# The last batch's attention in two passes of queries, with three quarters of its expert routing beside the second pass

## The chip, the cores and the metric

The kernel runs on one core of one Trainium2 chip. All arithmetic is in 32-bit floats. The metric is the device time of the whole kernel in microseconds (us): the median of the runs shown is 2341.13 us (three runs, 2332.34 to 2346.16).

## What is computed

Four batches of 2048 tokens, 256 features, go through an attention layer and a layer of experts, each between two layer norms, with a residual. Cut to what matters:

```python
# attention, per batch and head (16 heads of 16): z are 1-number projections of keys and queries
out_i = sum_j max(0, 1 - |z_i - z_j| / b_h) * v_j          # then / T
x = x + layernorm(out)
# experts: 8192 tokens h = layernorm(x), 64 experts, top 8, capacity 128 per expert in token order
shared = (silu(h @ Wg) * (h @ Wu)) @ Wd * sigmoid(h @ w_gate)   # width 512
probs = softmax(h @ gate_w); w, idx = top_k(probs, 8); w = w / sum(w)
y = sum over the 8 of  w * expert_e(h)      # only where the token is among the first 128 of expert e
x = x + layernorm(y + shared)
```

The capacity is handed out in token order over all batches, so an expert's list is only known when every token ahead has been routed.

## The kernel before, in words

**Foreground: attention.** A unit `t` of the loop at the end of `sandwich_kernel` is one head `h` and one tile `s` of 128 keys against all 2048 queries of a batch; there are `NU` = 256 units a batch, 1024 in all, and 64 units (4 heads, 16 key tiles) make a phase. For a unit, `score` writes `hat` = |q + k| over 128 keys x 2048 queries on ScalarE (L1558), or with two VectorE instructions (L1553, L1555) when VectorE's account `spare` is in credit; then VectorE makes min(hat, 1) - 1 (L1562). `product` multiplies `hat` by the head's values on TensorE (L1588): four matmuls a unit, each 128 keys x 32 value columns x 512 queries, one per block `c` of 512 queries. A matmul uses only 32 of the array's 128 columns, those of quarter `j`, the unit's head within its phase; block `c` is issued `c` units late, so that the four matmuls of one turn of the loop (units t, t-1, t-2, t-3) lie in four different quarters:

```python
def product(t):
    for c in range(4):
        tt = t - c
        ...
        nc.tensor.matmul(pa[k, c][32 * j:32 * j + 32, :], lhsT=vt[b, s]..., rhs=hat[tt][0][:, c * BK:(c + 1) * BK], ...)
```

After 128 units (8 heads) `evict` moves the four accumulators from PSUM to a tile `ct`, which goes to DRAM (`cx_d`) in batches 0 to 2 and stays in SBUF in batch 3. Queries are loaded broadcast to all partitions by `load_q` (L1539, 512 KB each), from 13 buffers called "big" that the hats share.

**Background: a planner.** Everything else is queued as small tasks in the class `Background`, in one list whose order is the priority. `bg.step()` is called once a unit. It goes through the list and emits each task whose predecessors are some steps old (`LAG`), whose buffers are free ("slot", "bank", "half"), and whose engine has budget left. Budgets are in us of the planner's own costs per step: `CAP` is 0.88 for TensorE, 0.75 for VectorE and 0.4 for ScalarE from batch 2 on. Each engine runs what it is given in the order given. `bg.flush(tasks)` emits the named tasks, and all that they depend on, at once and without regard to age. `bg.drain()` runs the planner alone after the attention, with a budget of 1.0.

**What is queued, and when.** `finish(b)` is queued 8 units into batch b + 1, for b = 0 to 2. It has the parts `front(c)` for four chunks of 512 tokens (load, transposes, layer norms, gate logits), `tail()` (softmax, top 8 and the codes of the tokens, 128 x 64 each, transposed into `scT`), `keep` (L706), `first` (L713 and L715: rounds of MAX8 and MATCH_REPLACE8 over `scT` that pick the earliest tokens) and `shared(c)`, the shared expert of a chunk: 16 matmuls of 512 columns (L573), Silu (L587), products (L589), 16 matmuls of 256 columns (L602), and a store of the result to `y_d` (L619). A matmul in 32-bit floats is two records in the trace, so a chunk of the shared expert is 32 records of each kind. `early` queues the 64 experts of the first half of the tokens (L1041 gather, L1047 to L1064, L1066 scatter with addition), ahead of `finish(2)` in the list. The "slot" buffers are ten; four of them go to the experts and are not handed back.

**After the attention.** Batch 3's own `finish` is written by hand: `front_last` (L721 to L891) for its four chunks, then `keep`, `first` over 1088 columns, `merge` (L963, L965), `ranking` (L1096 to L1186), and 15 items of experts for the second half (`item`: gather L1217, matmuls L1223 to L1240, 28 scatters L1258). All of these scatters add into `y_d` on top of the shared expert of batch 2, so they wait for its stores:

```python
rest, bg.q = bg.q, []          # what the attention left over
...
bg.q = mine + rest             # mine: front_last, keep, first, merge, ranking
ys = stored[2]
... item(env, i, late + [i_] + ..., ks, ys, wl[i])
outs = shared_last(env, exps, gates, xts)      # shared expert of batch 3 (L911 to L938)
```

Last come the `final` tasks of 16 chunks (L1281 load of `y_d`, L1288 to L1307 layer norm, L1321 addition to the output): eight need only the first half's experts, eight wait for the last item's scatter.

Of the kernel before, what the change touches and what calls it, by code (L numbers as in the profile page):

```python
# [25 lines left out]
class Background:  # L26
# [8 lines left out]
    def __init__(self, make):  # L35
        self.make = make
        self.free = {}
        self.q = []
        self.t = 0
        self.debt = dict.fromkeys(self.CAP, 0.0)  # L40
        self.spent = dict.fromkeys(self.CAP, 0.0)
        self.alone = False
# [27 lines left out]
    def emit(self, k):  # L70
        for key, r in k.get.items():
            tag, _ = self.free[r].pop(0)
            k.env[key] = self.make(tag)
            k.env["tag", key] = (r, tag)
# [66 lines left out]
def sandwich_kernel(ctx: ExitStack, tc: tile.TileContext, x_in, wqT, bq, wkT, bk, wvT, bv, wprojT, log_bw,  # L141
# [38 lines left out]
    cx_d = [dram.tile([NG, P, T], F32, name=f"cx_d{b}") for b in range(B - 1)]  # L180
# [5 lines left out]
    ysh_d = dram.tile([T, F], F32, name="ysh_d")  # L186
# [28 lines left out]
    NS = NT // 2 * P  # L215
    scT = const.tile([P, NS + CAP], F32, name="scT")
# [9 lines left out]
    with ExitStack() as ph:  # L226
# [31 lines left out]
        bg = Background(make)  # L258
        bg.free["slot"] = [(f"s{i}", 0) for i in range(NSLOT)]
# [196 lines left out]
        def finish(b, after=()):  # L456
# [5 lines left out]
            xfree = []  # L462
            def front(c):
# [93 lines left out]
                a = bg.add("act", 0.25, gate, [a])  # L557
                gts = bg.add("dve", 0.1, lambda gt=gt: nc.vector.tensor_scalar(gt, gt, 0.5, 0.5, ALU.mult, ALU.add), [a])
                ready[c] = (done, gt, gts)

            def shared(c):
# [32 lines left out]
                for i2 in range(2):  # L594
# [15 lines left out]
                    if i2 == 0:  # L610
# [10 lines left out]
                                 yy, put=[] if b == NE else [ys], env=env)  # L621
                stored[b].append(free_ys)
                if b == NE:
                    bg.add("sp", 1.0, lambda ys=ys, c=c: nc.sync.dma_start(rows(ysh_d, c * CT, CH), chunkview(env[ys])),
                           [free_ys], put=[ys], env=env)

            def tail():


                lgv = lambda: env["lg"].rearrange("p (n e) -> p n e", e=E + 1)[:, :, :E]  # L630
                mkv = lambda: env["lg"][:, :NT * E].rearrange("p (n e) -> p n e", e=E)
                prv = lambda: env["pr"][:, :NT * E].rearrange("p (n e) -> p n e", e=E)
                mx = t8 = ts_ = None
                t0 = b * NT
                wide = lambda a: a.unsqueeze(2).to_broadcast([P, NT, E])

                def most():
                    nonlocal mx, t8, ts_
                    mx = small.tile([P, NT], F32, tag="mx", name=f"mx_{b}")
                    t8 = small.tile([P, NT, TOPK], F32, tag="t8", name=f"t8_{b}")  # L640
                    ts_ = small.tile([P, NT], F32, tag="ts", name=f"ts_{b}")
# [13 lines left out]
                for i in range(0, NT, 4):  # L655
                    a = bg.add("dve", 0.55, lambda i=i: top(i), [a])
                for i in range(0, NT, 4):
                    a = bg.add("dve", 0.78, lambda i=i: rep(i), [a])

                def sums():  # L660
# [6 lines left out]
                tabs.append(bg.add("sp", 1.0, lambda: nc.sync.dma_start(tabrows(b * T, NT)[:, :, F:TW], prv()), [a],  # L667
                                   put=["pr"], env=env))
                a = bg.add("dve", 1.2, lambda: nc.vector.scalar_tensor_tensor(
                    out=mkv(), in0=mkv(), scalar=0.0, in1=wide(code[:, t0:t0 + NT]), op0=ALU.is_lt, op1=ALU.mult), [a])  # L670
                ev = []
                for r in range(NT // 8):
                    pk = ("psc", r)

                    def tr(r=r, pk=pk):
                        for i in range(4):
                            t = r * 8 + 2 * i
                            nc.tensor.transpose(env[pk][:, i * P:(i + 1) * P],
                                                mkv()[:, t:t + 2, :].rearrange("p a e -> p (a e)"), ident)
                    t_ = bg.add("pe", 0.58, tr, [a], get={pk: "bank"}, put=["lg"] if r == NT // 8 - 1 else [], env=env)  # L680
                    ev.append(bg.add("dve", 0.68, lambda r=r, pk=pk: nc.vector.tensor_copy(
                        scT[:, r * BK:(r + 1) * BK], env[pk]), [t_] + chain[-1:], put=[pk], env=env))
                return ev

            for c in range(NCH):
                front(c)
            if b < NE:
                for c in range(NCH):
                    shared(c)
            a = tail()  # L690
            if b < NE - 1:
                a = first(a, CAP, NS + CAP)
                a = bg.add("dve", 0.2, lambda: nc.vector.tensor_copy(scT[:, NS:], codes), [a])
            elif b == NE - 1:
                a = early(first(a, CAP, NS + CAP), stored[0] + stored[1])
            else:
                a = keep(a, 0)
                a = first([a], LP, NS)
                a = bg.add("dve", 0.2, lambda: nc.vector.tensor_copy(scT[:, NS:NS + LP], codes[:, :LP]), [a])
            chain.append(a)  # L700
            if b == NE:
                for c in range(NCH):
                    shared(c)

        def keep(ev, i):
            return bg.add("sp", 1.0, lambda: nc.sync.dma_start(ck_d[i][:, :], scT[:, :NS]), ev)  # L706

        def first(ev, n, w):

            a = ev[-1]  # L710
            for r in range(n // 8):
                c8 = codes[:, r * 8:(r + 1) * 8]
                a = bg.add("dve", 1.25, lambda c8=c8: nc.vector.max(out=c8, in_=scT[:, :w]), ev + [a])  # L713
                if r < n // 8 - 1:
                    a = bg.add("dve", 1.25, lambda c8=c8: nc.vector.match_replace(  # L715
                        out=scT[:, :w], in_to_replace=c8, in_values=scT[:, :w], imm_value=0.0), [a])
            return a

        def load_last(env):

            return [bg.add("sp", 1.0, lambda c=c: nc.sync.dma_start(xres(env, c), rows(xf, (B - 1) * T + c * CT, CH)),  # L721
                           get={("x", c // 2): "big"} if c % 2 == 0 else {}, env=env) for c in range(NCH)]
# [4 lines left out]
        def front_last(env, lds, cts):  # L727
# [3 lines left out]
            ev, late, exps, gates, xts = [], [], [], [], []  # L731
# [16 lines left out]
            for c in range(NCH):  # L748
# [1041 lines left out]
```

## Time and profile before

| | us |
|---|---|
| median of the runs shown | 2341.13 |
| the profiled execution | 2339.91 |
| its span | 2338.0 |
| attention of batch 3 (window 1535 to 2039) | 504 |
| from the attention's end to the end of the span | 298 |

Over the span TensorE (PE) is busy 1952.5 us (84%), VectorE (DVE) 1996.1 us (85%), ScalarE (ACT) 1966.8 us (84%), GpSimd (POOL) 490.4 us (21%). PEld is TensorE's weight load, which overlaps its matmuls. In a row of the timeline the first two numbers are the start and the length in us; brackets give the time that the engine sat idle before it and what ended that. A line of groups gives out<-in with their shapes, the count, busy us in all, the mean in ns of one, and idle time ahead with its main releasers. A row of windows has, behind the length, the busy us and number of instructions of PE, PEld, DVE, ACT and POOL, then the granted TensorE clock, the DMA engines' share and GB/s.

### The profile page before, as it was taken

What the parts mean: (1) busy time and instruction counts of PE and PEld (TensorE: products, weight loads), DVE (VectorE), ACT (ScalarE), POOL (GpSimd) and SP (SyncE); (2) the same over time, 40 slices, a digit from 0 to 9 for tenths busy, and PEclk for the clock granted to TensorE, in tenths of its full rate; (3) what the DMA queues carried; (4) which work ended last, traced back from release to release, by engine and by line L of the source; (5) the groups of instructions that cost most, each with busy time, mean ns of one, the idle gap of its engine ahead of it and who ended that gap; (6) DMA issues with size and microseconds to landing.
All of it is one profiled execution on the core that took longest, in us unless ns stands there. A gap on an engine that the chain in (4) does not pass through costs nothing. (4 is left out here: it accounts for less than half of the span.)

```text
span 2338.0 us, 32679 instructions
## 1 busy us (share of the span) xinstructions
PE 1952.5 (84%) x12552; PEld 687.2 (29%) x12552; DVE 1996.1 (85%) x3102; ACT 1966.8 (84%) x1269; POOL 490.4 (21%) x339
## 2 busy tenths in 40 slices
PE   7898979888799899677899887878888889987783
PEld 4332323222223222112222222223332223364342
DVE  4799999898999889999989998989999979886335
ACT  2899999898999998999999998989999989742213
POOL 1001010010120000003200003446553234442463
PEclk9999999999999999989999998999999999988897
DMA  4243534427351202142302014465544243355758
GB/s 127 91 133 120 184 103 153 151 88 264 117 162 64 91 19 70 37 147 69 112 19 81 28 54 122 114 186 151 174 121 136 57 134 90 102 177 147 177 124 197
DMA packets 195078, 274.32 MB, mean 117 GB/s; under 512 B 24833, under 2 KB 165505, under 8 KB 194145
## 3 DMA queue, kind: packets, MB, share of 16 engines
q1 hardware_dynamic: 165680, 235.33, 31.2%
q0 software_dynamic: 23824, 31.70, 8.3%
q10 hardware_dynamic: 5408, 5.11, 0.7%
q8 instruction: 101, 1.65, 0.3%
q14 instruction: 65, 0.52, 0.1%
HBM read 189.18 MB, written 82.90 MB: 116 GB/s over the span
## 5 line engine op out<-in xcount | busy, mean ns | idle before, releaser
L1558 ACT ACTIVATE hat<-qb,nk 128x2048 f32<-128x2048 f32 x959 | 1837.3, 1995 | 112.8 <-DMA qb<-zq_d 57.5
L1588 PE MATMUL pa<-hat,v 128*32 128x512 f32 x8192 | 1115.3, 620 | 284.4 <-DVE hat L1562 272.3
L1562 DVE TENSOR_SCALAR hat<-hat 128x2048 f32<-128x2048 f32 x1024 | 1230.3, 1223 | 97.2 <-ACT hat L1558 91.3
L1588 PEld LDWEIGHTS pa<-hat,v 128*32 128x32 f32 x8192 | 186.2, 110 | 900.0 <-DVE hat L1562 652.6
L1066 POOL DMA_INDIRECT y_d<-s,ix x64 | 147.8, 2309 | 286.7 <-DVE s L1064 145.4
L573 PE MATMUL k<-s,sgu 128*128 128x512 f32 x352 | 198.4, 651 | 0.0
L1041 POOL DMA_INDIRECT s<-tab_d,ix x64 | 106.0, 1657 | 327.6 <-DMA qb<-zq_d 259.0
L499 POOL TENSOR_TENSOR rsc<-rsc,mhalf 128x2 f32<-128x2 f32 x24 | 53.4, 2225 | 521.2 <-DVE rsc L498 521.0
L602 PE MATMUL k<-sd,s 128*128 128x256 f32 x384 | 113.7, 428 | 16.9 <-DVE s L589 7.4
L442 PE MATMUL k<-s,s 128*32 128x512 f32 x768 | 102.4, 592 | 0.0
L602 PEld LDWEIGHTS k<-sd,s 128*128 128x128 f32 x384 | 72.2, 205 | 86.4 <-issue 47.8
L573 PEld LDWEIGHTS k<-s,sgu 128*128 128x128 f32 x352 | 54.8, 192 | 136.3 <-issue 121.2
L305 POOL TENSOR_TENSOR rsa<-rsa,mhalf 128x4 f32<-128x4 f32 x16 | 30.8, 1925 | 290.9 <-DVE rsa L304 285.6
L1553 DVE TENSOR_SCALAR hat<-qb,nk 128x2048 f32<-128x2048 f32 x65 | 83.1, 1279 | 0.1
L1555 DVE TENSOR_SCALAR hat<-hat 128x2048 int32<-128x2048 int32 x65 | 79.9, 1229 | 2.2
L350 PE MATMUL k<-h,s 128*128 128x256 f32 x256 | 73.0, 413 | 0.0
L713 DVE MAX8 codes<-scT 128x8 f32<-128x1152 f32 (+2 forms) x48 | 63.4, 1321 | 0.2
L350 PEld LDWEIGHTS k<-h,s 128*128 128x128 f32 x256 | 45.4, 195 | 54.4 <-issue 48.6
L715 DVE MATCH_REPLACE8 scT<-codes,scT 128x1152 f32<-128x1152 f32 (+2 forms) x44 | 57.6, 1310 | 0.0
L607 DVE TENSOR_SCALAR s<-k,gt 128x256 f32<-128x256 f32 x48 | 22.8, 480 | 36.5 <-PE k L602 32.0
L442 PEld LDWEIGHTS k<-s,s 128*32 128x32 f32 x768 | 31.6, 138 | 54.0 <-issue 53.2
L1258 POOL DMA_INDIRECT y_d<-v,ix x28 | 39.9, 1426 | 23.5 <-DMA y_d<-s 7.9
(319 smaller groups left out, 1643.2 us busy)
## 6 DMA issues: line engine op xcount, KB each, us to landing
qb<-zq_d SPq DMA_DIRECT2D x128, 512.0 KB, 5.5
s<-m_d SPq DMA_DIRECT2D x48, 512.0 KB, 4.8
s<-_attn_hidden_states_dram SPq DMA_DIRECT2D x28, 512.0 KB, 5.5
v_d<-h SPq DMA_DIRECT2D x48, 192.0 KB, 2.6
v<-v_d SPq DMA_DIRECT2D x48, 192.0 KB, 2.5
h<-fn_expert_gate_up_w_dram SPq DMA_DIRECT2D x32, 256.0 KB, 3.5
s<-fn_expert_gate_up_w_dram SPq DMA_DIRECT2D x32, 256.0 KB, 2.8
b<-y_d SPq DMA_DIRECT2D x16, 512.0 KB, 9.3
```

The lines of the kernel that those rows point to most:

```text
L350: nc.tensor.matmul(env[pk][:, i * F:(i + 1) * F], lhsT=xv[:, k, o:o + P], rhs=wv[:, k, :], start=(k == 0), stop=(k == KF - 1))
L442: nc.tensor.matmul(env[pz][c * CR:(c + 1) * CR, :], lhsT=xv[:, r, :], rhs=env[mp][:, k * 2 * F:(k + 1) * 2 * F], start=(r == 0 and k == 0) ...
L573: nc.tensor.matmul(env[p_], lhsT=sgu[:, k, o:o + P], rhs=featview(env[xT])[:, k, :], start=(k == 0), stop=(k == KF - 1))
L602: nc.tensor.matmul(env[py][:, i * F:(i + 1) * F], lhsT=env[acts[f // 2]][:, o:o + P], rhs=sd[:, f, :], start=(f == 0), stop=(f == NI - 1))
L713: a = bg.add("dve", 1.25, lambda c8=c8: nc.vector.max(out=c8, in_=scT[:, :w]), ev + [a])
L1041: g = bg.add("pool", 1.3, lambda: nc.gpsimd.indirect_dma_start(out=xg(), out_offset=None, in_=tab_d[half][:, :], in_offset=bass.IndirectOf ...
L1066: s = bg.add("pool", 1.9, lambda: nc.gpsimd.indirect_dma_start(out=y_d[half][:, :], out_offset=bass.IndirectOffsetOnAxis(ap=iv(), axis=0), ...
L1553: nc.vector.tensor_scalar(ht, qb[n][0], k, None, ALU.add)
L1555: nc.vector.tensor_scalar(hi, hi, 0x7fffffff, None, ALU.bitwise_and)
L1558: nc.scalar.activation(ht, qb[n][0], AF.Abs, bias=k)
L1562: nc.vector.tensor_scalar(ht, ht, 1.0, 1.0, ALU.min, ALU.subtract)
L1588: nc.tensor.matmul(pa[k, c][32 * j:32 * j + 32, :], lhsT=vt[b, s].rearrange("p a w -> p (a w)")[:, h // 2 * VW + p * D:h // 2 * VW + p * D ...
```

## The change

Batch 3 becomes two passes of 256 units each (so 1280 units in all): the first over queries 0 to 1535 (`LC` = 3 chunks), the second over queries 1536 to 2047. A unit of the first pass is 1536 queries wide with three matmuls, one of the second is 512 wide with one. In the second pass four heads share one buffer for queries and one for hats (`packed`). The background takes a step at every third unit of the second pass. At its start five "big" buffers become "slot" buffers until the end. `finish(3)` for chunks 0 to 2 is queued 8 units into the second pass, behind all that is still in the list; its routing is flushed at the end of the attention with `tabs + chain`, its `shared` is left in `rest` where not emitted. `front_last`, `shared_last` and `load_last` do chunk 3 alone; the last `first` is over 320 columns; the items' scatters wait for `stored[2] + stored[3]`. The last experts' `final` no longer adds the shared expert for chunks 0 to 2, which is in `y_d`. The first half's experts hand their four "slot" buffers back when done. The account `spare` has terms for the width.

```diff
+        QS = [(b, 0, T) for b in range(B - 1)] + [(B - 1, 0, LC * CT), (B - 1, LC * CT, T - LC * CT)]
+        NB = len(QS)
...
+        packed = lambda t: 4 * width(t) <= T
...
         def score(t):
...
-            hat[t] = take(f"hat_{b}_{h}_{s}")
-            ht = hat[t][0]
+            w = width(t)
+            if not packed(t):
+                hat[t] = take(f"hat_{t // NU}_{h}_{s}")
+            elif j == 0:
+                hat[t] = take(f"hat_{t // NU}_{h}_{s}")
+            else:
+                hat[t] = (hat[t - j][0][:, j * w:], hat[t - j][1])
+            ht = hat[t][0][:, :w]
...
-            if spare[0] >= 1.3:
+            if spare[0] >= 1.3 * sz:
...
-                spare[0] -= 3.6
+                spare[0] -= 3.6 * sz + 0.18 * (1 - sz)
             else:
-                nc.scalar.activation(ht, qb[n][0], AF.Abs, bias=k)
-                spare[0] += 1.9 - 1.17
+                nc.scalar.activation(ht, q, AF.Abs, bias=k)
+                spare[0] += (1.9 - 1.17) * sz + 0.14 * (1 - sz)
...
         def product(t):
             for c in range(4):
                 tt = t - c
-                if not 0 <= tt < B * NU:
+                if not 0 <= tt < NB * NU or c >= width(tt) // BK:
                     continue
...
+            n = LC if b == B - 1 else NCH
+            nt = n * CH
...
-            for c in range(NCH):
+            for c in range(n):
                 front(c)
...
+                lo, o = NS - nt * HP, NS if b < B - 1 else NS - nt * HP
+                a = keep(a, b - NE, lo, NS)
+                a = first([a], LP, lo, NS + LP if b > NE else NS)
...
-            if b == NE:
-                for c in range(NCH):
+            if b >= NE:
+                for c in range(n):
                     shared(c)
...
+            bg.add("pool", 0.0, lambda: None, scs0, put=[(k, i) for k in "ew" for i in range(2)], env=env)
...
+                if u == 0 and b == B:
+
+                    for i in range(5):
+                        bg.free["slot"].append(bg.free["big"].pop(0))
                 if u == 8 and b > 0:
                     finish(b - 1, after=[last[B - 1]["end"]])
...
                 was = bg.spent["dve"]
-                bg.step()
+                if b < B or u % 3 == 2:
+                    bg.step()
                 spare[0] -= bg.spent["dve"] - was
...
             bg.flush(tabs + chain)
+            bg.free["big"] += [x for x in bg.free["slot"] if x[0].startswith("b")]
+            bg.free["slot"] = [x for x in bg.free["slot"] if not x[0].startswith("b")]
...
-            late.append(keep(ev, 1))
-            a = first([late[-1]], LP, NS + LP)
+            lo = (NCH - LC) * 2 * P
+            late.append(keep(ev, B - 1 - NE, 0, lo))
+            a = first([late[-1]], LP, 0, lo + LP)
...
-            ys = stored[2]
+            ys = stored[2] + stored[3]
```

## The prediction, made before the result was known

> **What bounds the kernel now.** I read the groups of instructions first, then the table of windows for batch 3 and for the stages behind it, then the timeline at their borders. The groups:
>
> ```profile
> L1558 ACT ACTIVATE hat<-qb,nk 128x2048 f32<-128x2048 f32 x959 | 1837.3, 1995 | 112.8 <-DMA qb<-zq_d 57.5 <-PE pa L1588 49.6 <-DMA cx_d<-ct 3.1
> L1562 DVE TENSOR_SCALAR hat<-hat 128x2048 f32<-128x2048 f32 x1024 | 1230.3, 1223 | 97.2 <-ACT hat L1558 91.3
> L645 ACT ACTIVATE s<-s 128x1024 f32<-128x1024 f32 x3 | 3.2, 1060 | 0.0
> ```
>
> ScalarE's scores are 1837 of 2338 us and wait little: they set the pace of the attention. The windows, batch 3 and then the stages after it:
>
> ```profile
> 1535.00:2039.00 504.00, 431.83 (x2867) 148.58 (x2866) 453.20 (x650) 474.64 (x304) 217.82 (x117) 0.98 0.46 126
> 2040.00:2091.00 51.00, 43.96 (x226) 35.43 (x227) 42.74 (x186) 24.20 (x44) 22.66 (x26) 0.83 0.54 165
> 2091.00:2111.00 20.00, 18.31 (x43) 7.79 (x41) 18.95 (x23) 3.58 (x6) 4.41 (x8) 1.00 0.44 121
> 2111.00:2128.00 17.00, 7.79 (x19) 4.58 (x20) 15.95 (x69) 0.00 (x0) 0.00 (x0) 0.63 0.00 0
> 2128.00:2204.50 76.50, 56.40 (x191) 35.27 (x192) 30.87 (x129) 22.86 (x48) 25.30 (x21) 0.81 0.84 199
> 2204.50:2273.30 68.80, 58.25 (x267) 29.01 (x264) 23.79 (x73) 9.01 (x23) 50.02 (x38) 1.00 0.61 133
> 2273.30:2338.00 64.70, 28.98 (x89) 18.13 (x87) 33.60 (x104) 21.88 (x44) 20.67 (x16) 0.73 0.88 197
> ```
>
> In batch 3 a unit takes 504/256 = 1.97 us; ScalarE is busy 94%, VectorE 90%, TensorE 86%, so no engine has much to give. Behind it: front_last 51 us, first 20, merge and ranking 17, then 76 us in which nothing is more than three quarters busy, then scatters 69, then finals 65. What the 76 us wait for is in the timeline:
>
> ```profile
> 2128.21 2.60 POOL L1217 DMA_INDIRECT v<-tab_d,ix  x1 [29.26 <-DVE ix L1139]
> ...
> 2200.98 0.36 SPq L619 DMA_DIRECT2D y_d<-s  x1
> ...
> 2204.55 1.65 POOL L1258 DMA_INDIRECT y_d<-v,ix  x1 [7.89 <-DMA y_d<-s]
> ```
>
> The items begin at 2128, but the first scatter needs the last store of batch 2's shared expert. That work had been left over: by line, 64 of 128 records of L573 (two chunks) and 92 of 128 of L602 (three, nearly) run after 2039. So the background was already more than batch 3 could hold. Last, TensorE's run lengths:
>
> ```profile
> 74.45 1.06 PE L1588 MATMUL pa<-hat,v 128*32 128x512 f32 x6 [1.03 <-DVE hat L1562]
> ...
> 76.58 1.06 PE L1588 MATMUL pa<-hat,v 128*32 128x512 f32 x8
> ```
>
> Three matmuls (6 records) of a unit take as long as four, 1.06 us, and the run of 4 records at 71.31 takes 1.05: a run's length is that of one matmul, since the quarters of the array work side by side. Where matmuls share a quarter, at the end (2037.22, 12 records, 2.76 us), weight loads come 0.43 us apart, so a lone one takes 2 x 0.43 + 0.2.
>
> **Attention, ScalarE's side.** Every score of batch 3 becomes two. The elements are the same; what is added is one fixed cost per unit. Eight scores in a row took 15.25 us (1943.07), 1.906 each. From L645 (1.060 for 1024) to L1558 (1.995 for 2048) an element costs 0.91 ns, which leaves 0.13 us fixed; the 256-wide L811 (0.592, with a scale operand besides) would leave 0.36. [...] With 0.09 us a unit of background as now (474.6 - 464.7 and idle) the floor is 1.57 us a unit in the first pass (402 us), and 3 x 0.63 + 0.03 = 1.92 us for three units in the second (164 us): 566, or **+62**.
>
> **Attention, VectorE's and TensorE's side.** VectorE pays for one more instruction a unit too, not more than the 0.15 us of its smallest ones (L1097, one column) and not less than the 0.06 of the change's own account: 15 to 38 us. Three L1562 in a row took 3.50 us, 1.17 each, so 1536 wide is 0.95 with the fixed part and 512 wide 0.35. The background's half us a unit stays, so 0.95 + 0.5 in the first pass, and 3 x 0.35 + 0.75 = 1.8 in the second: beside ScalarE, not above. TensorE is worse off. A run of three matmuls costs what four cost, and a background step, which comes at every unit of the first pass, ends each run: so per unit 431.8/256 = 1.69 us of TensorE as before, against ScalarE's 1.57. Runs without a background matmul between can close up (16 records in 1.92 us, so 0.86 a unit, three quarters of that for three), so 1.69 is not a floor: between 1.57 and 1.85 I take 1.66, 425 us. In the second pass three lone matmuls arrive 0.63 us apart; if they overlap, they and the drain take 1.06, and the planner adds up to 0.88 per step, because it has a backlog: 1.94 and a hand-over, say 2.03 x 85.3 = 173 us. Bounds: 1.92 (ScalarE alone) to 2.3. Sum 425 + 173 = 598 against 504: **+94** (from +62 to +150). It lies on the path: ScalarE and TensorE are the pace. Query loads are the same bytes in more pieces on SP's queue, among the expert weights' loads; the 13.4 us that ScalarE waited for queries in batch 3 may double or vanish, within the bounds. New DMAs are the store and reload of the three chunks' context (3 MB) and three more stores to `ysh_d` (1.5 MB); moved with `front` are the loads of x and the stores to the output, `x1_d` and `tab_d`. The engines of the DMA were 46% busy in batch 3, and these land in 3 to 6 us with none waiting on them but background: nothing. finish(3)'s powers on GpSimd queue behind scatters of 2.3 us (L1066), which lengthens its chain, not the units.
>
> **What the second pass can take.** It has 83 background steps behind finish(3), so 83 x 0.88 = 73 us of TensorE by the planner's costs. Ahead in the list is what the first pass leaves, as now: 2.3 chunks of shared(2) at 16 x 1.05 + 8 x 1.07 = 25.4, that is 58, and some 7 of experts. finish(3)'s own 14 (three fronts of 4.3, two transposes) come behind: 79 against 73. Its chain is long, too: finish(2) needed from 1546 to 1785 us, 121 steps, for four chunks up to keep (L706), with experts ahead of it. For three that is some 95, and `first` over 832 columns is 15 instructions of 0.9 at 0.75 a step, 18 steps more: 113 against 83. So I expect its end flushed behind the attention, in plain order, with the engines waiting on each other: the routing tail 15 us (by batch 2's durations: five passes over 768 columns of 0.95, 24 MAX8 and MATCH_REPLACE8 of 0.2 to 0.3, an exponential with its 1.28 us table load), `first` 15 x 0.99 = 15 us, and about one front, 16 us: **46** (from 15 to 80). The three chunks of shared(3) stay in `rest`.
>
> **After the attention.** Flush 46; front_last for one chunk, 24 (the first chunk took 2040.96 to 2069.2, with three others between); `first` over 320 columns, 15 x 0.42 = 6, and a store ahead of it; merge and ranking 17. Ranking ends 95 us behind the attention; it is 88 now. Of now, 14 us of `first` and 27 of front_last go; the flush takes that back. The scatters now also wait for shared(3): three chunks of 32 x 0.46 + 32 x 0.33 = 25 us, 76 us of TensorE. It has slots (the experts' four come back), and runs beside the ranking, but its queue stands still while front_last's transposes wait for VectorE's flush. I put the last store at 125 and the first scatter at 128 behind the attention, now 164.5 (2204.5 - 2040): **-36**. The scatters are 28 x 1.73 + 10 x 1.31 = 62 us of GpSimd with the 0.30 between them, of 69 now; shared_last beside them shrinks from four chunks to one, which gives 3 at most. Finals: three additions of 1.22 us less (L1314) of 65, -3 at most; they are paced by 0.88 of the DMA engines. Together **-40** (from -80 to 0).
>
> **Sum.** 2339.9 + 94 - 40 = 2394; the median of the runs is 1.2 above the profiled execution, so **2395**. Batches 0 to 2 don't change.
>
> **Rivals.**
> 1. *The second pass takes it all* (faster). If shared(2) and the routing are done before the attention ends, and shared(3) by the ranking's end, nothing holds the scatters: 24 + 8 + 17 to the ranking, some 20 for shared(3), 4 for a first item, then 66 and 61: 200 instead of 298, with the attention at its floor, 2339.9 - 98 + 62 = 2304. It decides at the flush: under 15 us of it, and shared's last store (L619) within 80 us of the attention's end. For it: slots are freed and lags are counted in steps, which are shorter. Against it: the 79 against 73. Chance 0.17.
> 2. *A wash*: attention +65 to +75, behind it -60 to -75. 2335 to 2350. Chance 0.11.
> 3. *TensorE in the second pass doesn't overlap.* Lone matmuls, waiting for one hat each, take 1.06 one after another: 3.2 + 0.9 a step, 350 us instead of 173; with half the overlap 260. 2480 or more. Against it is the run of 4, 6 and 8 records in one time; but in those all hats but one were ready. Chance 0.12.
> 4. My case, 2355 to 2450: 0.60.
>
> About 0.5% (12 us) is what a measurement of this kernel can tell from no change. Slower by more: cases 3 and 4, 0.72; within: 0.11; faster: 0.17. The range for 8 in 10 cuts a tenth on each side, into cases 1 and 3: 2310 to 2460.
>
> **What would show it.** ScalarE's 512-wide score at 0.65 to 0.72 (fixed cost right). Batch 3's two passes at 425 and 173 us. A block of L713 and L715 over 832 columns behind the last L1588: there if the routing was flushed. All of L573 of batch 3 behind the attention. A first L1258 some 128 us behind it, released by a store of `y_d`; GpSimd nearly without a pause from there. I am wrong if the first pass runs at ScalarE's 1.57 with TensorE below 90%, or if the flush is short.

## The result, and the profile after

The changed kernel takes 2462.44 us (median of four runs, 2460.47 to 2465.01) against 2342.12 us beside it: 1.0521 of the time before, 95% interval 1.0486 to 1.0556. It is slower, as forecast, but by 120 us and not by 54; the range ended 2 us too low.

The groups by shape give ScalarE's scores, one line of code in its three widths:

```profile
L1597 ACT ACTIVATE hat<-qb,nk 128x2048 f32<-128x2048 f32 x716 | 1370.5, 1994 | 82.5 <-PE pa L1633 38.2 <-DMA qb<-zq_d 37.8 <-DMA cx_d<-ct 3.7
L1597 ACT ACTIVATE hat<-qb,nk 128x1536 f32<-128x1536 f32 x240 | 359.0, 1566 | 24.2 <-DMA qb<-zq_d 19.1 <-PE pa L1633 4.3 <-DMA cx_d<-ct 0.9
L1597 ACT ACTIVATE hat<-qb,nk 128x512 f32<-128x512 f32 x238 | 147.3, 713 | 4.6 <-PE pa L1633 4.5
```

The windows are the first pass, the second, the stretch to the first item's gather, from there to the first scatter, the scatters, and the finals:

```profile
1539.00:1962.00 423.00, 379.71 (x2257) 138.34 (x2254) 342.08 (x567) 359.37 (x294) 204.45 (x120) 0.98 0.53 134
1962.00:2127.00 165.00, 156.74 (x687) 45.08 (x685) 153.73 (x428) 151.89 (x245) 6.45 (x8) 1.00 0.26 76
2127.00:2247.00 120.00, 71.95 (x235) 44.61 (x235) 90.00 (x331) 28.11 (x50) 22.28 (x26) 0.74 0.44 114
2247.00:2327.80 80.80, 74.15 (x272) 43.76 (x271) 27.66 (x80) 12.69 (x27) 12.77 (x10) 1.00 0.53 152
2327.80:2397.00 69.20, 45.24 (x213) 22.57 (x211) 20.32 (x66) 6.25 (x17) 50.65 (x38) 0.87 0.59 130
2397.00:2458.70 61.70, 0.00 (x0) 0.00 (x0) 27.48 (x97) 16.59 (x32) 23.80 (x16) 0.50 0.91 206
```

Three stages carry the 120.7 us between the two spans. The last accumulator is moved out of PSUM at 2126.5 instead of 2040.0: +86.5. The first scatter comes 201.3 us behind that instead of 164.5: +36.8. From the first scatter to the end it is 130.9 instead of 133.5: -2.6. The middle one is where the forecast went astray: it had -36 there. Before the first scatter TensorE is busy 74 of 80.8 us, and the timeline shows with what. SyncE's stores of the shared expert:

```profile
2260.26 0.37 SPq L627 DMA_DIRECT2D y_d<-b  x1
2272.92 0.37 SPq L627 DMA_DIRECT2D y_d<-s  x1
2296.92 0.36 SPq L627 DMA_DIRECT2D y_d<-b  x1
2321.81 0.37 SPq L627 DMA_DIRECT2D y_d<-b  x1
```

and GpSimd's last row ahead of the first scatter, and that scatter:

```profile
2263.79 1.26 POOL L1337 DMA_DIRECT2D out_dram<-s  x1 [2.03 <-ACT s L1323]
2327.81 1.65 POOL L1274 DMA_INDIRECT y_d<-v,ix  x1 [62.76 <-DVE v L1265]
```

A chunk of the shared expert leaves every 12 to 25 us, and GpSimd, whose scatter waits for all of them, sits idle for 62.76 us, to 6.00 us behind the issue of the last. (The releaser in the brackets is a product of VectorE at 2327.19, of a later item, whose L1270 is still to come. The first rows to scatter, from L1270, stand at 2321.26, ahead of the store issued at 2321.81, so I take that store for what came last.) How so much came to be left shows in the gate and up matmuls (L581, 32 records a chunk) in the first pass, the second, and behind:

```profile
1539.00:1962.00 423.00, 8.49 (x16) 2.56 (x16) 0.98 0.53 134
1962.00:2127.00 165.00, 34.89 (x62) 9.22 (x62) 1.00 0.26 76
2127.00:2458.00 331.00, 68.36 (x146) 29.20 (x146) 0.79 0.58 144
```

In the first pass ran half a chunk, where batch 3 of the kernel before had run two. And the routing of batch 2 stood still: in the kernel before the weights of its tail were stored at 1772.0 (L667) and its codes at 1784.7 (L706); now

```profile
1995.98 0.37 SPq L675 DMA_DIRECT2D tab_d<-s  x1
2004.96 0.32 SPq L716 DMA_DIRECT2D ck_d<-scT  x1
```

34 us into the second pass.

### The profile page after: what moved, and what is told of

It reads as the page before. It is cut to its first block, busy times and chain, and to the rows that moved or that the text cites. A ratio compares the mean times of both kernels' runs of the same rounds, so it can differ in the third digit from the quotient of the medians.

```text
span 2458.7 us, 33199 instructions
## 1 busy us (share of the span) xinstructions
PE 2044.1 (83%) x12552; PEld 704.0 (29%) x12552; DVE 2042.2 (83%) x3444; ACT 1993.2 (81%) x1470; POOL 473.7 (19%) x333
## 3 DMA queue, kind: packets, MB, share of 16 engines
q1 hardware_dynamic: 170784, 240.05, 30.9%
## 5 line engine op out<-in xcount | busy, mean ns | idle before, releaser
L1597 ACT ACTIVATE hat<-qb,nk 128x2048 f32<-128x2048 f32 (+2 forms) x1194 | 1876.6, 1652 | 111.3 <-DMA qb<-zq_d 57.0
L1633 PE MATMUL pa<-hat,v 128*32 128x512 f32 x8192 | 1212.7, 622 | 253.5 <-DVE hat L1603 240.5
L1603 DVE TENSOR_SCALAR hat<-hat 128x2048 f32<-128x2048 f32 (+2 forms) x1280 | 1250.0, 1008 | 78.6 <-ACT hat L1597 72.0
L1633 PEld LDWEIGHTS pa<-hat,v 128*32 128x32 f32 x8192 | 207.3, 110 | 923.5 <-DVE hat L1603 667.4
L581 PE MATMUL k<-s,sgu 128*128 128x512 f32 x384 | 215.5, 649 | 8.7 <-DVE b L597 8.7
L581 PEld LDWEIGHTS k<-s,sgu 128*128 128x128 f32 x384 | 60.6, 192 | 154.3 <-issue 129.9
L1592 DVE TENSOR_SCALAR hat<-qb,nk 128x2048 f32<-128x2048 f32 (+2 forms) x86 | 91.4, 1062 | 0.1
L1594 DVE TENSOR_SCALAR hat<-hat 128x2048 int32<-128x2048 int32 (+2 forms) x86 | 87.2, 1014 | 3.0
L309 POOL TENSOR_TENSOR rsa<-rsa,mhalf 128x4 f32<-128x4 f32 x16 | 30.9, 1931 | 288.6 <-DVE rsa L308 283.3
L1081 DVE TENSOR_SCALAR s<-k,s 128x256 f32<-128x256 f32 x64 | 30.8, 482 | 44.9 <-PE k L1078 44.7
L724 DVE MAX8 codes<-scT 128x8 f32<-128x1152 f32 (+3 forms) x56 | 65.3, 1165 | 0.5
L726 DVE MATCH_REPLACE8 scT<-codes,scT 128x1152 f32<-128x1152 f32 (+3 forms) x51 | 59.1, 1160 | 0.0
L328 PE MATMUL k<-ident,s 128*128 128x128 f32 x248 | 39.7, 299 | 19.2 <-DVE s L313 18.4
```

What stands on the lines that cost most here:

```text
L581: nc.tensor.matmul(env[p_], lhsT=sgu[:, k, o:o + P], rhs=featview(env[xT])[:, k, :], start=(k == 0), stop=(k == KF - 1))
L724: a = bg.add("dve", cost, lambda c8=c8: nc.vector.max(out=c8, in_=scT[:, lo:hi]), ev + [a])
L1592: nc.vector.tensor_scalar(ht, q, k, None, ALU.add)
L1594: nc.vector.tensor_scalar(hi, hi, 0x7fffffff, None, ALU.bitwise_and)
L1597: nc.scalar.activation(ht, q, AF.Abs, bias=k)
L1603: nc.vector.tensor_scalar(ht, ht, 1.0, 1.0, ALU.min, ALU.subtract)
```

## The experiments

All runs at a glance. The attention's end is the start of the last move out of PSUM.

| kernel | of the time before (95%) | attention ends | first scatter behind it |
|---|---|---|---|
| before | 1 | 2040.0 | 164.5 |
| changed | 1.0521 (1.0486 to 1.0556) | 2126.5 | 201.3 |
| e1, no gate's wait | 1.0390 (1.0360 to 1.0419) | 2143.3 | 149.7 |
| e4, tail ahead of shared | 1.0448 (1.0416 to 1.0480) | 2139.2 | 163.3 |
| e2, before + gate's wait | 1.0119 (1.0096 to 1.0143) | 2039.1 | 188.9 |
| e3, before + split | 1.0272 (1.0248 to 1.0296) | 2135.7 | 121.0 |
| e6, e1 less shared(3) | 1.0306 (1.0283 to 1.0330) | 2141.8 | 132.6 |
| e7, e1 + routing first | 1.0225 (1.0210 to 1.0241) | 2137.9 | 111.0 |
| e14, changed + routing first | 1.0439 (1.0420 to 1.0458) | 2127.5 | 184.7 |
| e16, e7 + more steps | 1.0274 (1.0255 to 1.0293) | 2183.2 | 76.5 |
| e11, e3 + quartets | 1.0235 (1.0220 to 1.0250) | 2132.6 | 125.0 |
| e8, before + slots back | 0.9908 (0.9889 to 0.9926) | 2032.9 | 151.0 |
| e17, before + guards | 1.0004 (0.9992 to 1.0016) | 2036.6 | 166.4 |
| e10, before + shared ahead (1/4) | 1.0060 (1.0041 to 1.0079) | 2038.9 | 128.9 |
| e12, before + shared ahead (1/8) | 0.9965 (0.9952 to 0.9978) | 2038.5 | 123.8 |
| e18, e8 + e12 | 0.9977 (0.9965 to 0.9988) | 2033.5 | 126.1 |

**My first theory: slots.** The diff has a line that I had read past. The planner's order, written out while a kernel is built, shows what it does (steps of the planner; the first pass is 768 to 1023; "free" is slots left):

```
            kernel before                changed kernel
tail's first step takes a slot   870    waits: free 0     1025
  and gives it back              889
shared(2), chunk 0, first block  897    866, takes the last slot
  second block takes a slot      940    waits: free 0     1025
```

With the gate's Tanh among what the tail waits for, the tail can start five steps later than without (869 in e4 below, 864 in e1), and by then chunk 0 of the shared expert has taken the last of ten slots. It needs a second one before it can give any back, and the tail needs one before it can give back the one with the logits: both wait for slots from elsewhere. The experts of the first half, which need no more slots, run ahead meanwhile. At step 1024 they are done and hand their four back, and at the next step the five big buffers are there too. The tail's slot is one of the experts' four, so it was these, and not the five, that ended the wait.

Removing the line:

```diff
                 a = bg.add("act", 0.25, gate, [a])
-                lgs.append(a)
```

> The changed kernel without one line of the diff: the tail of a batch's routing no longer waits for the gate's Tanh on ScalarE. Slot theory: with that line the router's tail of batch 2 asks for its work tile five planner steps after the shared expert's first block has taken the last free slot, and both stand still until five more slots come at the second pass. Without it the tail's weights are stored near 1755 us instead of 1996, one to one and a half chunks of the shared expert of batch 2 go into the first pass, the first scatter comes 140 to 160 us behind the attention instead of 201, and the time is 2390 to 2420 us. Rival, the second pass has too little room whatever is left for it: the backlog moves, the end doesn't; 2455 to 2470.

Measured 2428.22 us, 1.0390. The mechanism is right and its size half of what I expected. The weights of the tail are stored at 1735.0, the codes at 1757.1; 64 records of gate and up (two chunks) run in the first pass. The first scatter comes 149.7 us behind the attention, as expected, but the attention itself ends 17 us later: what the planner can now put there has to be done there. About 30 us are gained, not 60. The line has its use, though: the tail writes over the logits that the Tanh reads. In e1 the last three Tanhs start behind such a write, which released them:

```profile
2183.11 0.41 ACT L560 ACTIVATE gt<-b 128x4 f32<-128x4 f32 x3 [7.10 <-DVE b L676]
```

So e1, and e6 below, give the price of the line and are no repair. In e7 and e16 nothing but the order of the list puts the Tanhs first; e4 keeps the line.

Is it the slot, or the wait for ScalarE? Keeping the line, and making the shared expert wait for the tail's first step:

```diff
                 a = bg.add("dve", 1.2, most, lgs + chain[-1:], get={"pr": "slot"}, env=env)
+                held.append(a)
...
-                    a = bg.add("pe", 1.05, ..., done + [a], get=get, env=env)
+                    a = bg.add("pe", 1.05, ..., done + held + [a], get=get, env=env)
```

> The changed kernel with the gate's wait kept, and the shared expert's first block of each chunk made to wait for the first step of the router's tail, so that the slot goes to the tail. Slot theory: as without the line, 2390 to 2420 us. If it is the wait on ScalarE itself that costs (the tail late by an engine's queue), this stays at 2455 to 2470.

Measured 2437.19, 1.0448: its interval ends below the changed kernel's and touches e1's. So the slot is at least a good part of it (0.7%, 17 us); the rest, if it is one, is the line's own delay, which the next run shows without any slot conflict, in the kernel before:

```diff
                 a = bg.add("act", 0.25, gate, [a])
+                lgs.append(a)
```

> The kernel before with that one line added. Slot theory: in the kernel before a slot more is free at that point, so the tail is five planner steps late and nothing stands still: within 8 us of 2342. If the wait itself costs: 2360 or more.

Measured 2362.06, 1.0119: the second of my cases, the wait itself costs. In this kernel the tail takes its slot at step 875 and not 870, and nothing stands still. That is not because a slot more is free, as I had it: the tail takes the last one there too, and the shared expert only asks later (896). Yet 56 instead of 64 records of gate and up run before the attention ends, the last store of the shared expert is issued at 2224.3 instead of 2201.0, and the first scatter follows it at 2228.0. A slip of five steps costs 24 us between the profiled spans, 28 by the ratio. As I read it, what just fails to get in before the attention's end queues behind the routing after it; no run here separates that.

**The split by itself.** The kernel before with `score`, `load_q`, `product` and `evict` of the change, no `finish(3)`, and front_last for all four chunks, out of both passes' accumulators; the background steps at every third unit of the second pass, as in the change (cut):

```diff
+        QS = [(b, 0, T) for b in range(B - 1)] + [(B - 1, 0, LC * CT), (B - 1, LC * CT, T - LC * CT)]
...
-                if u == 8 and b > 0:
+                if u == 8 and 0 < b < B:
...
```

> The kernel before with the last batch's attention in two passes (1536, then 512 queries) and nothing else: its routing of all four chunks and their shared expert stay behind the attention. Prices the split: attention longer by 86 us as in the changed kernel. If the first scatter then waits only for the ranking, because the shared expert of batch 2 ends in the second pass, the tail gives back 30 to 50 us and the time is 2380 to 2400. If the tail is bound by the work of its own four chunks, nothing comes back: 2420 to 2435.

Measured 2396.64, 1.0272. The attention pays 96 us, the second pass ends the shared expert of batch 2 (last store 2133.3), and 43 us of the wait come back. So the split costs 2.7%, and what else the change does costs another 2.5%. Most of what the split costs shows on TensorE. The windows of its attention matmuls alone, first the kernel before, then the split's two passes (us busy, records; two records are one matmul):

```profile
1535.00:2040.00 505.00, 277.69 (x2052) 42.60 (x2050) 0.98 0.46 126
```

```profile
1539.00:1976.00 437.00, 258.77 (x1494) 40.21 (x1494) 1.00 0.50 130
1976.00:2136.00 160.00, 94.94 (x542) 17.35 (x542) 1.00 0.26 62
```

271 ns a matmul before, 346 and 350 ns in the two passes: the same matmuls take 76 us more. The timeline of the second pass says why:

```profile
2040.90 1.06 PE L1618 MATMUL pa<-hat,v 128*32 128x512 f32 x6
2041.89 1.13 PE L574 MATMUL k<-s,sgu 128*128 128x512 f32 x2
2042.94 1.91 PE L1618 MATMUL pa<-hat,v 128*32 128x512 f32 x12
2044.79 1.13 PE L574 MATMUL k<-s,sgu 128*128 128x512 f32 x2
```

Three matmuls between two background matmuls take 1.06 us, as four did in the kernel before (8 records at 76.58). And TensorE is the fullest engine in both passes, above all in the second (windows as in the result):

```profile
1539.00:1976.00 437.00, 403.47 (x2288) 141.15 (x2288) 355.75 (x624) 383.70 (x310) 191.41 (x114) 1.00 0.50 130
1976.00:2136.00 160.00, 159.64 (x760) 50.17 (x759) 145.19 (x382) 136.49 (x226) 12.44 (x8) 1.00 0.26 62
```

In the changed kernel the matmuls of the second pass take longer still, 403 ns each (106.1 us for 527 records): batch 2's late tail and `first` share VectorE with the hats there, in instructions of up to 1.22 us (L677 at 1996.88, L724 at 2039.99). The run of three below takes 1.72 us; VectorE finished its three hats one after another, from 2044.33 to 2045.42:

```profile
2044.80 1.72 PE L1633 MATMUL pa<-hat,v 128*32 128x512 f32 x6 [0.48 <-DVE hat L1603]
```

**Four together again.** In the second pass, the four heads' matmuls of one key tile issued at every fourth unit:

```diff
+                if packed(tt) and j < 3:
+                    continue
+                for i in range(3 if packed(tt) else 0, -1, -1):
+                    b, g, p, s, j, h = unit(tt - i)
                     nc.tensor.matmul(pa[k, c][32 * j:32 * j + 32, :], ..., rhs=hat[tt - i][0][...], ...)
```

> The split alone (2397 us) with the second pass's four matmuls of one key tile, which lie in four different quarters of the array, issued together at every fourth unit instead of one at each unit. If matmuls that no longer run side by side are what the split costs (354 us of TensorE for these matmuls against 278 before), the second pass's fall from 97 to 70 or 80 us, and the attention ends 10 to 25 us earlier: 2372 to 2388. Rival, ScalarE's one fixed price more per unit holds the pass: 2390 to 2400.

A miss: 2394.05, 1.0235, an interval that touches the split's, and a time in the rival's range. The matmuls of the second pass fell from 94.9 to 89.7 us only, and the attention ends 3 us earlier. Its timeline has both sorts of quartet:

```profile
2043.54 1.06 PE L1622 MATMUL pa<-hat,v 128*32 128x512 f32 x8
2044.53 1.13 PE L574 MATMUL k<-s,sgu 128*128 128x512 f32 x2
...
2051.80 2.05 PE L1622 MATMUL pa<-hat,v 128*32 128x512 f32 x8 [0.27 <-DVE hat L1588]
```

The quartet at 2043.54, with no wait ahead of it, takes 1.06, and the next matmul starts 0.99 us behind its start, as behind the three of the split (2040.90 to 2041.89); the one at 2051.80, behind a wait for VectorE's hat, takes 2.05. The rival's engine is not the full one here: ScalarE is busy 137 of the second pass's 157 us, TensorE 154. So the 76 us of lost overlap are measured. That they are what makes up the attention's 96 is argued, from how full TensorE is; the run that was to show it by taking them back did not.

**What waits behind the attention.** The changed kernel without the gate's wait, and without the shared expert of chunks 0 to 2 of batch 3:

```diff
-            if b >= NE:
+            if b == NE:
                 for c in range(n):
                     shared(c)
...
-            ys = stored[2] + stored[3]
+            ys = stored[2]
```

> The changed kernel without the gate's wait (2428 us, first scatter 150 us behind the attention), and the shared expert of chunks 0 to 2 of the last batch left out altogether (their rows of the sum are zeros plus the experts). If the first scatter is late because it waits for those three chunks, which before the change were not in its way: it comes 120 to 130 us behind the attention, and the time is 2395 to 2408. Rival, the flushed routing and the ranking are what sets it: 2420 to 2430.

Measured 2410.89, 1.0306: 0.8% (20 us) under e1, the first scatter 17 us earlier, at 132.6. So leaving the three chunks out altogether takes away 17 of the 29 us by which e1's first scatter comes later than the split's; the rest is elsewhere. Next, the order of the list (all of `finish(3)`, its shared expert too, ahead of what was left):

```diff
+                    had, bg.q = bg.q, []
                     finish(b - 1, after=[last[B - 1]["end"]])
+                    bg.q = bg.q + had if b == B else had + bg.q
```

> The changed kernel without the gate's wait, and the last batch's routing put ahead of all that is still in the list at the second pass, instead of behind it. The flush behind the attention (60 us) should fall under 30, but shared expert work of batch 2 is pushed behind the attention by as much. If the shared expert's last store sets the first scatter, the time stays at 2420 to 2436. If the flush sets it, 2395 to 2405.

Measured 2391.17, 1.0225, 1.6% (39 us) under e1, and under the range that I had given to the flush: the flush it is. The stretch from the attention's end to the first gather, in e1:

```profile
2143.50:2254.00 110.50, 66.48 (x218) 39.92 (x216) 88.63 (x324) 24.04 (x44) 22.33 (x27) 0.75 0.48 124
```

and in e7:

```profile
2138.00:2210.70 72.70, 53.11 (x175) 30.77 (x174) 64.96 (x231) 22.18 (x41) 18.91 (x19) 0.84 0.68 161
```

From the gather to the first scatter it is 39 and 38 us. e7 leaves no less of the shared expert behind the attention (88 records of gate and up against 92, 128 of the down matmuls, L609, against 96). In e1 the first 60 us (2143.3 to 2203.4, where `first` over 832 columns ends) are one flushed chain, each instruction waiting for the last; the shared expert's matmuls come behind it in TensorE's queue, and TensorE idles 44 of 110 us. In e7 the chain is mostly done beside the second pass, and the stretch is 38 us shorter. The same order with the gate's wait kept:

> The changed kernel as it is (with the gate's wait), and the last batch's routing put ahead of the list. If the two faults are independent, the order alone is worth the 37 us it gave without the gate's wait: 2420 to 2430. Slot theory: with the wait the shared expert of batch 2 stands still through the first pass as before, and now also behind the routing in the second; all four of its chunks and the three of batch 3 end behind the attention, and the first scatter comes 200 us or more behind it: 2455 to 2490.

Measured 2441.85, 1.0439, between my two cases: the order gives 0.8% here and 1.6% without the wait. The shared expert does stand still through the first pass (16 records), and the two faults share a wait in part. Taken in this order, the list is worth 19 us and the gate's wait 50 (e14 against e7), and not 39 and 31.

Has the second pass room left? e7 with a background step at every second unit (`u % 2 == 1`; the loads of the last chunk are queued 24 units before the end and not 36):

> The changed kernel without the gate's wait and with the routing first (2391 us), and a background step at every second unit of the second pass instead of every third. TensorE is 99% busy in that pass, so what is added there should lengthen the pass by as much as it takes from behind: 2385 to 2400. If the pass had room left that the planner does not use, 2365 to 2380.

Measured 2402.23, 1.0274, slower than e7 and 2 us above my range. The first scatter now comes 76.5 us behind the attention, and the attention ends 45 us later. No room: in e7's second pass TensorE is busy 168.3 of 170 us.

**A part of the diff that helps.** The diff also hands the first half's four slots back when its experts are done. That alone, in the kernel before (with the guard e >= 4 on the scatter that a gather waits for, also in the diff, cut):

```diff
+            bg.add("pool", 0.0, lambda: None, scs0, put=[(k, i) for k in "ew" for i in range(2)], env=env)
+            bg.q.insert(0, bg.q.pop())
...
-                ld = bg.add("sp", 1.0, load, a + gs[e - 2:e - 1], ...)
+                ld = bg.add("sp", 1.0, load, a + (gs[e - 2:e - 1] if e >= 2 else []), ...)
```

> The kernel before with one part of the diff alone: the first half's experts hand their four slots back when they are done. They end 55 us behind the attention there, when the shared expert of batch 2 is bound by TensorE and the order of the list, not by slots: within 10 us of the kernel before. If slots hold that shared expert behind the attention too: 2310 to 2330.

Measured 2318.65, 0.9908: the second of my cases, not the one that I had argued for. This version beats both kernels. The guards let one more expert start at once, so they were tried alone:

> The kernel before with only the two index guards that the diff adds to the list of the first half's experts (for the first four experts no earlier one is waited for; in the kernel before the third waited for the first one's scatter, by a negative index). Where the slots handed back gave 0.991 of the time before: if it was this earlier start (the attention ended 7 us earlier), 2318 to 2328 here; if it was the slots that come back behind the attention, 2335 to 2342.

Measured 2338.33, 1.0004: the guards by themselves give nothing, so it is the slots. (7 of the 21 us between e8's span and that of the kernel before stand already at the attention's end, where the slots are not back yet. What these are is open; e17's attention ends 3 us earlier and its time is the same.) Where the slots act shows in the kernel before, in SyncE's loads for the `final` tasks:

```profile
2099.45 1.57 SPq L1281 DMA_DIRECT2D s<-y_d  x3
2159.89 3.50 SPq L1281 DMA_DIRECT2D s<-y_d  x3
...
2170.72 11.39 SPq L1281 DMA_DIRECT2D s<-y_d  x2
```

and, between 2128 and 2204, in VectorE's waits (us in total, times, longest) and two of its rows:

```profile
DVE v L1292 <- DMA s<-y_d: 16.2, 3, 7.9
DVE s L607 <- PE k L602: 14.1, 7, 3.6
```

```profile
2187.05 1.41 DVE L1292 BATCH_NORM_STATS2 v<-s 128x6 f32<-128x256 f32 x4 [7.35 <-DMA s<-y_d]
2188.37 0.67 DVE L589 TENSOR_TENSOR s<-s,pa 128x512 f32<-128x512 f32 x1
```

With the slots back seven loads go out at once, at 2088.94, and between 2040 and 2184 VectorE waits for none of them. SyncE's rows for the same loads:

```profile
2088.94 5.93 SPq L1287 DMA_DIRECT2D s<-y_d  x7
2152.34 0.37 SPq L1287 DMA_DIRECT2D s<-y_d  x1
```

In the kernel before the loads had to wait for slots; VectorE then stood at a final's statistics (L1292) until its load had landed, with the products of the shared expert's last chunk (L589) queued behind, and that chunk's store is what the scatters wait for. It leaves at 2180.2 now, 2201.0 before.

**Order of the list in the kernel before.** If the last store of batch 2's shared expert holds the scatters, it can be put ahead of a part of the first half's experts:

```diff
+                    had, bg.q = bg.q, []
                     finish(b - 1, after=[last[B - 1]["end"]])
+                    k = 3 * len(had) // 4 if b == B - 1 else len(had)
+                    bg.q = had[:k] + bg.q + had[k:]
```

> The kernel before, with the routing and shared expert of batch 2 put ahead of the last quarter of the first half's experts that are in the list at that point, instead of behind them all. If the last store of that shared expert is what holds the scatters of the kernel before, the first comes 20 to 30 us earlier and the rest of the first half's experts runs behind the attention without being in its way: 2315 to 2330. Rival, the displaced experts take GpSimd and TensorE from the items: 2335 to 2350.

Measured 2351.69, 1.0060: a miss, slower, the rival's side. The first scatter does come 36 us earlier, but the displaced experts' gathers and scatters run among the items', which take 115 instead of 69 us. With 7/8 for 3/4:

> The kernel before with the routing and shared expert of batch 2 ahead of the last eighth of the first half's experts in the list instead of the last quarter (which came to 1.006 of the time before: first scatter 36 us earlier, but the scatters spread from 69 to 115 us among the displaced experts' own). With half as many displaced, the first scatter some 25 us earlier and the scatters 75 to 85 us: 2320 to 2338. If any displaced expert costs what it gives: 2338 to 2350.

2329.63, 0.9965: a gain, but of 0.4%; the scatters take 91 us (2162.3 to 2253.4). And both together, the slots and this order:

> The kernel before with the slots handed back (0.991) and the shared expert of batch 2 ahead of the last eighth of the experts (0.9965). If both shorten the same wait for the shared expert's last store, they do not add up: 2312 to 2326. If they add up: 2300 to 2312.

2331.14, 0.9977: a miss, and less than the slots alone. The first scatter does come 24 us earlier than in e8 (2159.6), but the scatters take 94 us and not 68, and from the last of them to the end it is 75 us and not 65. So the order's gain is there, and its price is higher.

## Why the prediction was right in direction and wrong in size

- **ScalarE's fixed price: right.** The floors of 1.57 and 1.92 us and the +62 stand on 0.63 us for a 512-wide score and 1.48 for 1536, which no run before the change shows: its rows gave a fixed part of 0.13 to 0.36. In the changed kernel fourteen 512-wide scores in a row took 8.68 us (1962.29), 0.62 each, and three 1536-wide 4.50 (1707.98), 1.50 each. The 512-wide ones' busy mean is 0.713, inside the 0.65 to 0.72 that I had set as the test.
- **TensorE, and the attention's +94: right**, at +86. The passes took 423 and 165 us against 425 and 173, and most runs of three took 1.06 us (rival 3, with lone matmuls one after another, had 350 for the second pass). Mostly beside batch 2's late tail and `first` is there something of rival 3: 1.72 us for a run (1996.35, 2044.80). "A run of three matmuls costs what four cost" is what e3 measures as 76 us. I had given ScalarE's floor and TensorE about equal weight; in the second pass TensorE is the fullest (157 of 165 us, with VectorE at 154 and ScalarE at 152; 168 of 170 in e7). The 173 counts a drain within the 1.06 us of a run; no run shows one by itself. What the rows show is that a background matmul begins 0.99 us behind the start of a run, whether that has three matmuls (2040.90 in e3) or four (2043.54 in e11).
- **"Ahead in the list is what the first pass leaves, as now: 2.3 chunks": the step that failed.** It left 3.5 chunks of gate and up, all four of down, and batch 2's tail and `first`. I had costed the planner by budgets and priorities and not by buffers: one more predecessor made the tail ask for a slot five steps later, when there was none. e4 shows the slot (17 us) and e1 the whole line: with it out the changed kernel is about 30 us faster, of the 66 by which the forecast fell short. Behind the attention I had put shared(3) alone, 76 us of TensorE; it was 109 (68.4 + 40.7).
- **The flush: right in kind, 62 us (to 2188.2) against 46**, since nearly two fronts were flushed and not one. Its price was mis-sized too. I had it take back what `first` and front_last give; but what is flushed also stands ahead of the shared expert's matmuls in TensorE's queue. e7 prices the flush behind the list at 39 us, e14 at 19.
- **First scatter at 128: wrong, 201.** With the slots and the order mended it comes at 111 (e7), and the time is 2391, which is near the 2395 forecast, but for a kernel that was not the one changed.
- **Scatters and finals: right**, -2.6 us against at most -3 for each.
- **Rival 1 (2304) fails at the second pass.** e16 has its short wait, 76.5 us, and pays for it with 45 us of attention: its floor of +62 assumed room on TensorE that was not there.
- **What I did not look for:** the slots handed back are worth -0.9% in the kernel before. Of the parts of the diff that were tried alone they are the only one that gains, and the profile before had the row (VectorE waiting 16.2 us for finals' loads) in a stage where I had read only "nothing is more than three quarters busy".

So the 120 us of the changed kernel, by the runs: the split some 64 (e3); the gate's wait with its slots some 31 (e1); the routing behind the rest of the list some 39 (e7 against e1); and from these about 11 come back, since e7, with both mended and the routing moved, ends 0.5% under the split alone. That last is all that moving the routing gives, and the intervals of e7 and e3 just part (1.0241, 1.0248). These are differences of ratios from separate comparisons, good to 6 to 11 us each by their intervals, and the 31 and the 39 depend on which fault is taken out first (e14 has 50 and 19). Open: why the two faults overlap as they do (e14), and how much of the 0.6% between e4 and e1, whose intervals touch, is the late tail alone.

## What to carry to other kernels

Where a planner gives out buffers, follow the buffers as well as the engines: an added predecessor that costs nothing on any engine can hand the last buffer to a task that cannot finish without another. Work moved beside a loop whose tightest engine was full was not hidden: TensorE was busy 168.3 of 170 us in e7, and e16, with more steps beside the same loop, lengthened the attention by 45 us. And the narrower tiles cost TensorE, which had lived on overlap between tiles, 76 us (e3), while the records' own durations did not grow: 613 ns the mean of one before, 606 and 603 in e3's two passes. In a tail, find the store that the next stage waits for, and then what stands ahead of its producers in each engine's queue.

## What was not expected of the hardware

Four 32-column matmuls in four quarters took 1.06 us together at 2043.54 in e11, and 2.05 us at 2051.80 in the same kernel, behind a wait for VectorE's hat; grouping them won 5 us of TensorE (94.9 to 89.7) where 15 to 25 were expected. And an engine that was 40% busy (VectorE, 30.9 of 76.5 us in the kernel before) was the one that held that stage: it stood 16.2 us at loads that nothing on the path needed, with the instructions behind them that the path did need.
